# Passes over the edges of a graph network: a fixed instruction order, one-hots for eight chunks at once, lagging additions, more gather buffers

## The chip, the cores and the metric

The kernel runs on one core of one Trainium2 chip, in one launch. The metric is device time in microseconds (us), the median of several runs. A core has five instruction queues, each in order: TensorE (PE, with its weight loads shown as PEld), VectorE (DVE), ScalarE (ACT), GpSimd (POOL) and SyncE (SP). They wait for each other, and for transfers, on semaphores.

## The reference

A graph network on 12,500 nodes with 128 features and 200,000 edges, whose edges come sorted by destination. It has four layers, each followed by a residual and a layer norm. Every layer holds one sum over edges:

```python
num = segment_sum(vals[:, None] * gx[cols], rows)     # layer 0: weighted, by source
agg = segment_sum(feats[src] * norm[:, None], dst)    # layer 1: then a mixture of 64 experts
h   = segment_sum(xs[s], d)                           # layer 2
agg = segment_sum(x[src], dst)                        # layer 3: then two small matrices
```

For every edge a row of 128 (in layer 0, 129) numbers is fetched by the index of one end and added to the row of the other end. The kernel scales the rows of the table, and the sums, by the nodes' own factors outside of these passes; only layer 0 has a weight for each edge. Layer 0's pass also counts the edges that each node receives.

## The kernel before, in words

Nodes lie on partitions, 128 to a node tile, 98 tiles. In its first 2769 us the kernel groups the edges by the node tile of their source, and by that of their destination, and makes *chunks*: 128 edges, one on each partition, whose sums all go to one node tile. There are 1664 chunks in each grouping, so 6656 chunk steps in the four passes. For each chunk it holds the row to gather for every edge (`row`), the edge's place within the node tile (`loc`) and the tile's offset in the table of sums (`off`).

A pass is one call of `edge_sums`. The steps of one chunk, with their lines:

- POOL issues an indirect DMA (L386) that gathers 128 rows from DRAM into the buffer `g`, one of 16 in the pool `gat`. [...]
- In layer 0 alone, ACT multiplies the rows by their weights into `ms` (L390), a ring of `NM` = 8.
- DVE makes a one-hot (L394): a 128x128 matrix that has a 1 where the edge's place is the column, by comparing `iota` with one number for each partition. It has 4 buffers in the pool `hot`.
- PE multiplies the one-hot with the rows (L396), in fp32, which the trace records as two weight loads and two matmuls, into one of 6 PSUM tiles. The product has the sum of each node's edges in the node's own row.
- DVE adds the PSUM tile to the sums `ACC` (L398), at an offset that it has in a register. The offsets are loaded four at a time (L380).

In layer 0 each four chunks are followed by the counting of received edges: DVE makes one-hots `lo` and `hi` for four blocks at once (L402, L405), in tiles of the pool `hot` too, and PE multiplies them (L408) into one PSUM tile that is summed up through the pass.

The program is written chunk by chunk, in the order above. A scheduler sets the order of each engine's instructions. On DVE it puts the one-hot of a chunk some three to four chunks ahead of that chunk's addition, so that in the steady state the queue goes: addition, one-hot of a later chunk, addition, one-hot, and so on. A pool gives its buffers in turn: the gather waits until the matmul (in layer 0, ACT's product) that read its buffer 16 chunks back is done, the one-hot until the matmul four one-hots back is done, and the matmul until the addition that read its PSUM tile six back is done. Before the first chunk of a pass the sums are set to zero (L367, 10.68 us of DVE).

The rest of the kernel (layer norms, the experts between the second and third pass, batch norm) isn't touched by the change.

Of the kernel before, what the change touches and what calls it, by code (L numbers as in the profile page):

```python
# [20 lines left out]
N = 12500                   # nodes; node n lies on partition n % 128 of node tile n // 128  # L21
D = 128
NT = 98                     # node tiles
NP = NT * P
LAST = N - (NT - 1) * P     # nodes in the last tile
E = 200000                  # edges
EC = 1564                   # edges per partition, as loaded
EP = P * EC
NBLK = EP // P              # blocks of 128 edges
NK = 13  # L30
NCH = NK * P                # chunks: a block of edges and a node tile that it reaches
PAD = NP                    # behind every node tile
W0 = D + 2                  # columns of the sums: features, weight sum, edge count
NE = 64                     # experts
# [5 lines left out]
SL = TT * NTT               # rows per expert  # L40
# [3 lines left out]
GM = 7                      # node tiles per group  # L44
# [3 lines left out]
def gnn_kernel(ctx: ExitStack, tc: tile.TileContext, a, out: bass.AP):  # L48
# [6 lines left out]
    # ---- constants  # L55
# [34 lines left out]
    # ---- edges by destination, in chunks: row to gather, place within the node tile  # L90
# [19 lines left out]
    # ---- small helpers on per-node numbers  # L110
# [23 lines left out]
    def bc(v, n):  # L134
        return v[:, :, None].to_broadcast([P, v.shape[1], n])
# [19 lines left out]
    # ---- the edges, grouped by the node tile of their source, and of their destination  # L155
# [4 lines left out]
    def chunks(pool, pps, cum, i, off):  # L160
        """The blocks of edges that each node tile reaches; for each chunk its tile and its block."""
# [46 lines left out]
    def rank_and_store(hi, hv, cum, pack, pos_i, i):  # L208
        """Counting sort by node tile: each edge's place, and its row stored there."""
# [38 lines left out]
    def take_chunks(wk, pps, tl, blk_i, i, row, loc, wgt):  # L248
        """The chunks' edges, one per partition; in a packed row are source, destination, weight."""
        key = i             # grouped by source (0) or by destination (1)  # L250
# [22 lines left out]
    with tc.tile_pool(name="ea", bufs=1) as pa, tc.tile_pool(name="eps", bufs=1, space=PSUM) as pps, \  # L273
# [28 lines left out]
        for i, hi, off in ((0, s_hi, s_off), (1, d_hi, e_off)):  # L302
            hv = pa.tile([P, NT + 2], F32, name=f"hv{i}")
            V.memset(hv, 0.0)
            if i == 1:
                # destinations out of the order of their node tiles
# [13 lines left out]
        # hyperbolic points: table rows are gamma * x_hyp and gamma - 1  # L320
# [26 lines left out]
        # destinations that come grouped by node tile are stored as they are; others are ranked first  # L347
# [11 lines left out]
    # ---- sums over the edges of each node: gather rows, add by a one-hot product  # L359
    def edge_sums(ACC, table, row, loc, off, wgt=None):  # L360
# [3 lines left out]
        with tc.tile_pool(name="gat", bufs=16) as gp, tc.tile_pool(name="hot", bufs=4) as hp, \  # L364
                tc.tile_pool(name="msg", bufs=1) as mp, tc.tile_pool(name="eps", bufs=6, space=PSUM) as ep, \
                tc.tile_pool(name="ops", bufs=1, space=PSUM) as op_:
            V.memset(ACC, 0.0)  # L367
            NM = 8
# [10 lines left out]
            for c0 in range(0, NCH, 4):  # L379
                _, at = nc.values_load_multi_w_load_instructions(  # L380
                    off[0:1, c0:c0 + 4], engines=[mybir.EngineType.DVE], min_val=0, max_val=(NT - 1) * W0,
                    skip_runtime_bounds_check_because="clamped to the last node tile on the chip")
                for i in range(4):
                    c = c0 + i
# [8 lines left out]
                    oh = hp.tile([P, P], F32, name="oh")  # L393
                    V.tensor_scalar(oh, iota, loc[:, c:c + 1], None, op0=OP.is_equal)  # L394
                    ps = ep.tile([P, cols], F32, name="ps")
                    T.matmul(ps, oh, m, start=True, stop=True)  # L396
                    o = ACC[:, ds(at[i], cols)]
                    V.tensor_tensor(o, o, ps, OP.add)  # L398
                if weighted and c0 < EC:
                    # edges that each node receives  # L400
                    lo = hp.tile([P, 4, P], BF16, name="lo")
                    V.tensor_tensor(lo, bc(d_lo[:, c0:c0 + 4], P),  # L402
# [376 lines left out]
```

## Time and profile before

| | |
|---|---|
| median of 3 runs | 14288.24 us (14288.1 to 14297.87) |
| span of the profiled execution, first to last instruction | 14129.2 us |
| median less that span | 159.0 us |
| grouping of the edges, up to the first gather of a pass | 2769 us |
| pass 0 (layer 0, weighted, with the counting) | 2769 to 5215: 2446 us |
| pass 1 (layer 1) | 5385 to 7772: 2387 us |
| experts and batch norm | 7772 to 9086: 1314 us |
| pass 2 (layer 2) | 9086 to 11474: 2388 us |
| pass 3 (layer 3) | 11611 to 13998: 2387 us |
| busy share of the span: PE, PEld, DVE, ACT, POOL | 38%, 27%, 43%, 7%, 62% |
| mean granted TensorE clock | 0.725 |

A line of the groups reads: line of the kernel, engine, operation, output<-inputs, size, count, then busy time in all and the mean of one in ns, then the idle time of the engine just before these instructions, and what ended most of that idle time. "issue" there means that the profile shows nothing that the engine waited for. A line of the timeline reads: start, busy time (both us), engine, line, operation, count, and in brackets the idle time before it with its releaser. Matmuls are pipelined and their ends in the trace are modelled: what tells that a matmul has ended is the instruction that waited for it.

### The profile page before, as it was taken

How to read it: one execution, taken by the hardware profiler on the slowest of the kernel's cores; microseconds unless marked ns; L12 is line 12 of the kernel's file. 1: busy time of each engine (PE TensorE's matmuls, PEld its weight loads, DVE VectorE, ACT ScalarE, POOL GpSimd, SP SyncE). 2: the span in 40 equal slices, each digit the busy share in tenths (PEclk: the TensorE clock that was granted, in tenths of full speed). 3: DMA queues.
4: the chain of work that ended last, by engine and by line, in shares of the span. 5: the costliest groups of instructions: out<-in, count | busy, mean ns of one | idle time of the engine just before them, and what ended most of it. 6: DMA issues, size and time to landing. Idle time of an engine off the chain costs nothing. (4 is left out here: it accounts for less than half of the span.)

```text
span 14129.2 us, 98197 instructions
## 1 busy us (share of the span) xinstructions
PE 5383.5 (38%) x18927; PEld 3844.2 (27%) x18927; DVE 6094.2 (43%) x17635; ACT 1011.7 (7%) x2245; POOL 8749.1 (62%) x8647
## 2 busy tenths in 40 slices
PE   0000000144444433554444385254554425544445
PEld 0000000033333322333333263133333313333334
DVE  9999200144545454333333522533333353333335
ACT  0000000022222220000000121000000000000001
POOL 2888777666666645666666503366666636666663
PEclk9999999999999997555555697555555555555556
DMA  1000000122222211111111143111111111111111
GB/s 48 8 1 1 1 1 1 63 79 46 46 46 46 46 37 50 46 46 46 47 46 45 40 139 89 41 46 46 46 46 46 46 46 46 47 46 47 46 46 47
DMA packets 502257, 619.52 MB, mean 44 GB/s; under 512 B 171448, under 2 KB 379834, under 8 KB 501532
## 3 DMA queue, kind: packets, MB, share of 16 engines
q0 software_dynamic: 277248, 470.82, 13.9%
q1 hardware_dynamic: 164876, 112.21, 2.5%
q10 hardware_dynamic: 59536, 30.17, 0.8%
q14 instruction: 422, 3.46, 0.1%
q8 instruction: 175, 2.87, 0.1%
HBM read 511.43 MB, written 101.18 MB: 43 GB/s over the span
## 5 line engine op out<-in xcount | busy, mean ns | idle before, releaser
L386 POOL DMA_INDIRECT g<-table,e_row x4992 | 4709.0, 943 | 2943.7 <-PE ps L396 1390.8
L396 PE MATMUL ps<-g,oh 128*128 128x128 f32 x9984 | 3471.6, 480 | 4140.4 <-issue 1703.7
L398 DVE TENSOR_TENSOR ACC<-ACC,ps 128x128 f32 (+1 forms) x6656 | 1915.0, 288 | 5966.0 <-PE ps L396 4069.3
L396 PEld LDWEIGHTS ps<-g,oh 128*128 128x128 f32 x9984 | 2402.4, 311 | 5209.6 <-issue 2658.5
L241 POOL DMA_INDIRECT packed<-pack,src_i x1564 | 1991.2, 1273 | 693.0 <-issue 474.1
L386 POOL DMA_INDIRECT g<-table,s_row x1664 | 1637.5, 984 | 796.5 <-issue 524.7
L394 DVE TENSOR_SCALAR oh<-iota,e_loc 128x128 f32<-128x128 f32 x4992 | 1440.9, 297 | 3.9 <-DMA table<-tb 3.1
L396 PE MATMUL ps<-ms,oh 128*128 128x130 f32 x3328 | 995.1, 457 | 664.0 <-issue 366.3
L396 PEld LDWEIGHTS ps<-ms,oh 128*128 128x128 f32 x3328 | 778.0, 321 | 812.6 <-issue 555.3
L260 PE MATMUL tp<-ident,g 128*128 128x128 f32 x65 | 21.7, 442 | 2124.7 <-DVE g L257 2110.1
L390 ACT ACTIVATE ms<-g,s_w 128x129 f32<-128x129 f32 x1664 | 646.7, 401 | 1793.5 <-PE ps L396 824.7
L260 PEld LDWEIGHTS tp<-ident,g 128*128 128x128 f32 x65 | 11.3, 200 | 2135.1 <-DVE g L257 2098.0
L256 DVE COPY g<-gt 128x384 f32<-128x384 f32 x26 | 17.3, 666 | 1250.9 <-DMA gt<-packed,blk_i 1250.7
L654 POOL DMA_INDIRECT yk<-ybuf,come x196 | 188.3, 961 | 593.4 <-DMA ybuf<-ye 533.7
L394 DVE TENSOR_SCALAR oh<-iota,s_loc 128x128 f32<-128x128 f32 x1664 | 435.3, 292 | 0.2
L408 PE MATMUL d_ps<-hi,lo 128*128 128x98 bf16 x1564 | 189.6, 271 | 634.4 <-DVE hi L405 411.6
L408 PEld LDWEIGHTS <-lo 128*128 128x128 bf16 x1564 | 144.1, 124 | 714.5 <-issue 422.0
L233 DVE TENSOR_TENSOR_SCAN inc<-keep,oh 128x1683 f32<-128x1683 bf16 x92 | 336.9, 3662 | 2.5
L598 POOL DMA_INDIRECT buf<-ACC,goi x196 | 197.4, 1007 | 146.7 <-issue 92.5
L238 DVE TENSOR_REDUCE pos<-oh 128x17 f32<-128x1683 f32 x92 | 285.1, 3099 | 2.5
L402 DVE TENSOR_TENSOR lo<-d_lo,iota_b 128x512 bf16<-128x512 bf16 x391 | 267.7, 685 | 0.0
L636 PE MATMUL ph<-bT,w 128*128 128x392 f32 x512 | 215.5, 524 | 71.7 <-DVE bT L630 66.3
(305 smaller groups left out, 3791.3 us busy)
## 6 DMA issues: line engine op xcount, KB each, us to landing
g<-table,e_row POOLq DMA_INDIRECT x4992
g<-table,s_row POOLq DMA_INDIRECT x1664
buf<-zero SPq DMA_DIRECT2D x56, 448.0 KB
xt<-buf ACTq DMA_DIRECT2D x64, 392.0 KB
ybuf<-ye SPq DMA_DIRECT2D x64, 392.0 KB
packed<-pack,src_i POOLq DMA_INDIRECT x1564
w<-in_L_gnn_W SPq DMA_DIRECT2D x128, 128.0 KB
table<-tb SPq DMA_DIRECT2D x28, 448.0 KB
```

Source lines behind the costliest of these rows:

```text
L233: V.tensor_tensor_scan(inc.rearrange("p b k -> p (b k)"), keep.rearrange("p b k -> p (b k)"), oh.rearrange("p b k -> p (b k)"), 0.0, OP.mu ...
L238: V.tensor_reduce(pos, oh.rearrange("p b k -> p k b"), AX.X, OP.add)
L241: st = G.indirect_dma_start(out=rows, out_offset=bass.IndirectOffsetOnAxis(ap=pos_i[:, k:k + 1], axis=0), in_=pack[:, k, :], in_offset=None)
L386: G.indirect_dma_start(out=g, out_offset=None, in_=table[:, :], in_offset=bass.IndirectOffsetOnAxis(ap=row[:, c:c + 1], axis=0))
L390: S.activation(m[:, 0:width], g, AF.Copy, scale=wgt[:, c:c + 1])
L394: V.tensor_scalar(oh, iota, loc[:, c:c + 1], None, op0=OP.is_equal)
L396: T.matmul(ps, oh, m, start=True, stop=True)
L398: V.tensor_tensor(o, o, ps, OP.add)
L402: V.tensor_tensor(lo, bc(d_lo[:, c0:c0 + 4], P), iota_b[:, None, :].to_broadcast([P, 4, P]), OP.is_equal)
L408: T.matmul(d_ps, lo[:, i, :], hi[:, i, :], start=(c0 + i == 0), stop=(c0 + i == EC - 1))
L598: st = G.indirect_dma_start(out=buf[:, :], out_offset=bass.IndirectOffsetOnAxis(ap=goi[:, i, k:k + 1], axis=0), in_=A3[:, t0 + i, 0:D], in ...
L636: T.matmul(ph[:, 0:HALF], w1[:, j * P:(j + 1) * P], bT[:, q * HALF:(q + 1) * HALF], start=True, stop=True)
```

## The change

Only `edge_sums` changes in what it does; elsewhere comments alone go.

- The order of DVE, PE, ACT and POOL inside the pass is the written one (`manual_schedule`), no longer the scheduler's.
- One-hots: one `tensor_tensor` makes those of eight chunks (128 x 8 x 128), from `loc` and `iota`, both spread to that shape, where a `tensor_scalar` made one. The pool `hot` has four tiles of eight. The groups 0 and 1 are made ahead of the first chunk; group g+2 is made at the first chunk of group g.
- An addition stands four chunks behind its matmul in DVE's order (`LAG`). The offsets are still loaded four at a time, before the first addition that needs them.
- The counting's one-hots have a pool of their own (`cnt`, two of each), and the counting of four blocks stands ahead of the four chunks, not behind them.
- 32 gather buffers, not 16; 7 PSUM tiles, not 6; a ring of 12 weighted products, not 8.

The instruction lists of the two kernels show on DVE, per eight chunks: one one-hot instruction; in layer 0 `lo`, `hi`; an offset load and four additions; in layer 0 `lo`, `hi`; an offset load and four additions. POOL's gathers are the same in number and order and differ in what they wait for. PE has the same matmuls, with the counting's ahead of the chunk's own.

```diff
-        with tc.tile_pool(name="gat", bufs=16) as gp, tc.tile_pool(name="hot", bufs=4) as hp, \
-                tc.tile_pool(name="msg", bufs=1) as mp, tc.tile_pool(name="eps", bufs=6, space=PSUM) as ep, \
+        with tc.tile_pool(name="gat", bufs=32) as gp, tc.tile_pool(name="hot", bufs=4) as hp, \
+                tc.tile_pool(name="cnt", bufs=2) as cp, \
+                tc.tile_pool(name="msg", bufs=1) as mp, tc.tile_pool(name="eps", bufs=7, space=PSUM) as ep, \
...
-            NM = 8
+            NM = 12
...
-            for c0 in range(0, NCH, 4):
-                _, at = nc.values_load_multi_w_load_instructions(
-                    off[0:1, c0:c0 + 4], engines=[mybir.EngineType.DVE], min_val=0, max_val=(NT - 1) * W0,
+            def hots(g):
+                t = hp.tile([P, NB, P], F32, name="oh")
+                V.tensor_tensor(t, bc(loc[:, g * NB:(g + 1) * NB], P),
+                                iota[:, None, :].to_broadcast([P, NB, P]), OP.is_equal)
+                return t
+
+            def count(c0):
+                lo = cp.tile([P, 4, P], BF16, name="lo")
+                V.tensor_tensor(lo, bc(d_lo[:, c0:c0 + 4], P),
+                                iota_b[:, None, :].to_broadcast([P, 4, P]), OP.is_equal)
+                hi = cp.tile([P, 4, NT], BF16, name="hi")
+                V.tensor_tensor(hi, bc(d_hi[:, c0:c0 + 4], NT),
+                                iota_b[:, None, 0:NT].to_broadcast([P, 4, NT]), OP.is_equal)
                 for i in range(4):
+                    T.matmul(d_ps, lo[:, i, :], hi[:, i, :], start=(c0 + i == 0), stop=(c0 + i == EC - 1))
+
+            LAG = 4
+            with tc.manual_schedule(engines={mybir.EngineType.DVE, mybir.EngineType.PE,
+                                            mybir.EngineType.Activation, mybir.EngineType.Pool}):
+                made = {g: hots(g) for g in (0, 1)}
+                sums, at = {}, {}
+
+                def add(c):
+                    if c % 4 == 0:
+                        _, at[c // 4] = nc.values_load_multi_w_load_instructions(
+                            off[0:1, c:c + 4], engines=[mybir.EngineType.DVE], min_val=0, max_val=(NT - 1) * W0,
...
+                    o = ACC[:, ds(at[c // 4][c % 4], cols)]
+                    V.tensor_tensor(o, o, sums.pop(c), OP.add)
+
+                for c in range(NCH):
+                    if c % NB == 0 and c // NB + 2 < NG:
+                        made[c // NB + 2] = hots(c // NB + 2)
+                    if weighted and c % 4 == 0 and c < EC:
+                        count(c)
                     g = gp.tile([P, width], F32, name="g")
...
-                    oh = hp.tile([P, P], F32, name="oh")
-                    V.tensor_scalar(oh, iota, loc[:, c:c + 1], None, op0=OP.is_equal)
                     ps = ep.tile([P, cols], F32, name="ps")
-                    T.matmul(ps, oh, m, start=True, stop=True)
-                    o = ACC[:, ds(at[i], cols)]
-                    V.tensor_tensor(o, o, ps, OP.add)
-                if weighted and c0 < EC:
-                    lo = hp.tile([P, 4, P], BF16, name="lo")
...
+                    T.matmul(ps, made[c // NB][:, c % NB, :], m, start=True, stop=True)
+                    sums[c] = ps
+                    if c >= LAG:
+                        add(c - LAG)
+                for c in range(NCH - LAG, NCH):
+                    add(c)
```

More of the change, by code (lines that the diff above doesn't have):

```diff
@@ L357, in gnn_kernel @@
         take_chunks(wk, pps, info[1][3], info[1][4], 1, e_row, e_loc, None)
+    NB = 8
+    NG = NCH // NB
     def edge_sums(ACC, table, row, loc, off, wgt=None):
@@ L378, in edge_sums @@
                 d_ps = op_.tile([P, NT], F32, name="d_ps")
-            for c0 in range(0, NCH, 4):
-                _, at = nc.values_load_multi_w_load_instructions(
-                    off[0:1, c0:c0 + 4], engines=[mybir.EngineType.DVE], min_val=0, max_val=(NT - 1) * W0,
-                    skip_runtime_bounds_check_because="clamped to the last node tile on the chip")
-                for i in range(4):
-                    c = c0 + i
+            def hots(g):
[3 more added lines that the diff above has]
+                return t
@@ new lines, in edge_sums @@
+            LAG = 4
[7 more added lines that the diff above has]
+                            off[0:1, c:c + 4], engines=[mybir.EngineType.DVE], min_val=0, max_val=(NT - 1) * W0,
+                            skip_runtime_bounds_check_because="clamped to the last node tile on the chip")
+                    o = ACC[:, ds(at[c // 4][c % 4], cols)]
[5 more added lines that the diff above has]
+                        count(c)
@@ L392, in edge_sums @@
                         m = g
-                    oh = hp.tile([P, P], F32, name="oh")
-                    V.tensor_scalar(oh, iota, loc[:, c:c + 1], None, op0=OP.is_equal)
                     ps = ep.tile([P, cols], F32, name="ps")
-                    T.matmul(ps, oh, m, start=True, stop=True)
-                    o = ACC[:, ds(at[i], cols)]
-                    V.tensor_tensor(o, o, ps, OP.add)
-                if weighted and c0 < EC:
-                    lo = hp.tile([P, 4, P], BF16, name="lo")
-                    V.tensor_tensor(lo, bc(d_lo[:, c0:c0 + 4], P),
-                                    iota_b[:, None, :].to_broadcast([P, 4, P]), OP.is_equal)
-                    hi = hp.tile([P, 4, NT], BF16, name="hi")
-                    V.tensor_tensor(hi, bc(d_hi[:, c0:c0 + 4], NT),
-                                    iota_b[:, None, 0:NT].to_broadcast([P, 4, NT]), OP.is_equal)
-                    for i in range(4):
-                        T.matmul(d_ps, lo[:, i, :], hi[:, i, :], start=(c0 + i == 0), stop=(c0 + i == EC - 1))
+                    T.matmul(ps, made[c // NB][:, c % NB, :], m, start=True, stop=True)
[4 more added lines that the diff above has]
+                    add(c)
             if weighted:
```

## The prediction, made before the changed kernel ran

> **What bounds the kernel now.** I began with the table of busy time cut into stretches, taken from the first gather to the last addition of each of the four passes over the edges. Its columns are the stretch, its length, busy time (and instructions) of PE, PEld, DVE, ACT and POOL, the granted TensorE clock, the DMA share and GB/s.
>
> ```profile
> 2769.00:5215.00 2446.00, 1147.73 (x4892) 919.00 (x4892) 1201.56 (x4116) 647.97 (x1665) 1637.51 (x1664) 1.00 0.23 56
> 5385.00:7772.00 2387.00, 1146.29 (x3328) 798.45 (x3328) 817.77 (x3324) 0.00 (x0) 1570.04 (x1665) 0.53 0.18 46
> 9086.00:11474.00 2388.00, 1185.91 (x3328) 804.68 (x3328) 808.40 (x3329) 0.00 (x0) 1569.46 (x1664) 0.52 0.18 46
> 11611.00:13998.00 2387.00, 1139.44 (x3328) 799.24 (x3328) 815.97 (x3326) 0.00 (x0) 1569.83 (x1664) 0.51 0.18 46
> ```
>
> The passes are 9608 of the 14129 us of span. No engine fills one: POOL is at 66%, DVE at 34 to 49%. 2387/1664 is 1.43 us a chunk, 2446/1664 is 1.47.
>
> Next the costliest groups, to see who waits:
>
> ```profile
> L386 POOL DMA_INDIRECT g<-table,e_row x4992 | 4709.0, 943 | 2943.7 <-PE ps L396 1390.8
> L396 PE MATMUL ps<-g,oh 128*128 128x128 f32 x9984 | 3471.6, 480 | 4140.4 <-issue 1703.7
> L398 DVE TENSOR_TENSOR ACC<-ACC,ps 128x128 f32 (+1 forms) x6656 | 1915.0, 288 | 5966.0 <-PE ps L396 4069.3
> L386 POOL DMA_INDIRECT g<-table,s_row x1664 | 1637.5, 984 | 796.5 <-issue 524.7
> L402 DVE TENSOR_TENSOR lo<-d_lo,iota_b 128x512 bf16<-128x512 bf16 x391 | 267.7, 685 | 0.0
> ```
>
> The addition waits for the matmul, the gather too (its buffer is free only when the matmul 16 chunks back is done). A gather takes 0.943 us and starts 1.25 us after the last where nothing holds it (9196.83 and 9198.08), so POOL's own pace is 1.25, and 0.18 us a chunk is lost to PE. The timeline of the steady state shows a tempting cause:
>
> ```profile
> 9199.29 0.29 DVE L398 TENSOR_TENSOR ACC<-ACC,ps 128x128 f32 x1 [1.75 <-PE ps L396]
> 9199.49 0.29 DVE L394 TENSOR_SCALAR oh<-iota,e_loc 128x128 f32<-128x128 f32 x1
> ...
> 9199.84 0.80 PE L396 MATMUL ps<-g,oh 128*128 128x128 f32 x2 [1.45 <-issue]
> 9200.73 0.29 DVE L398 TENSOR_TENSOR ACC<-ACC,ps 128x128 f32 x1 [0.94 <-PE ps L396]
> ```
>
> Addition, one-hot, matmul, addition: a loop of 1.44 us, just the pace. But the matmul at 9199.84 is not the one that the addition at 9200.73 takes. How far they stand apart is seen early in the pass, some 16 chunks in:
>
> ```profile
> 9106.50 0.76 PE L396 MATMUL ps<-g,oh 128*128 128x128 f32 x2 [0.44 <-DMA g<-table,e_row]
> ...
> 9107.83 0.76 PE L396 MATMUL ps<-g,oh 128*128 128x128 f32 x2 [0.56 <-DMA g<-table,e_row]
> ...
> 9109.08 0.77 PE L396 MATMUL ps<-g,oh 128*128 128x128 f32 x2 [0.49 <-DMA g<-table,e_row]
> ...
> 9110.23 0.77 PE L396 MATMUL ps<-g,oh 128*128 128x128 f32 x2 [0.39 <-DMA g<-table,e_row]
> ...
> 9112.54 0.29 DVE L398 TENSOR_TENSOR ACC<-ACC,ps 128x128 f32 x1 [5.10 <-issue]
> ...
> 9117.44 0.29 DVE L398 TENSOR_TENSOR ACC<-ACC,ps 128x128 f32 x1 [4.42 <-issue]
> ```
>
> Four matmuls start at the gathers' pace, and their sums come only 4.9 us apart. From there each addition is followed by one one-hot and one matmul start, so four stay begun and unfinished: that is where the four one-hot buffers stop. PE thus has work in hand all the time and still gives one chunk each 1.43 us. Then the end of the last pass:
>
> ```profile
> 13986.90 0.94 POOL L386 DMA_INDIRECT g<-table,e_row  x1 [0.30 <-issue]
> ...
> 13989.22 0.29 DVE L398 TENSOR_TENSOR ACC<-ACC,ps 128x128 f32 x1 [0.28 <-PE ps L396]
> ...
> 13989.62 0.28 DVE L398 TENSOR_TENSOR ACC<-ACC,ps 128x128 f32 x1
> ```
>
> Once the last gather is issued, chunks come 0.40 to 0.75 us apart (19 additions in 10 us, 0.53 on average), with the same one-hot buffers and order. So the order is not what keeps PE at 1.43; what it is the profile doesn't name.
>
> [...] the granted clock here is 1.00 in pass 0 and 0.51 to 0.53 in the others with nearly one pace, so the trace does not settle it. [...] gathers take 984 ns in pass 0, where the two-input count one-hots run, and 943 elsewhere. [...]
>
> **The change part by part.**
> One-hots: 6656 tensor_scalars go, 1440.9 + 435.3 = 1876 us of DVE. 832 tensor_tensors of 1024 elements come[...]. DVE per eight chunks is then 1.22 + 8 x 0.29 + two offset loads of some 0.34 = 4.2 us, in pass 0 with 2 x (0.685 + 0.560) 6.7, against 10 us of gathers. DVE doesn't bound; this saving lies beside PE's time and I cost it at nothing. Were DVE in the loop, it would be worth up to the 0.18 us a chunk, until POOL's 1.25 binds.
> Contention: the new one-hots have two SBUF inputs where the old had one. In pass 0 the count one-hots take 1.245 us per four chunks, 0.311 a gather, and the gather is 41 ns longer: 13%. The new ones are 1.224/8 = 0.153 us a gather, so 20 ns. Bounds: nothing, if POOL waits for PE anyway (0.18 us of slack a chunk covers it), and 6656 x 20 ns = 133 us if not. I take nothing.
> Order and lag: the addition trails by four chunks. It waits for a matmul four back, and behind it on DVE stand only one-hots needed eight or more chunks later. In pass 0 the count one-hots stand behind the addition five chunks back, and PE's count matmuls, now ahead of the chunk's own, wait for them: 1.25 us, covered by four chunks in hand (4 x 0.77 at least). One-hots of two groups now follow the 10.7 us clearing of the sums, so a pass's first matmul may be 2.4 us later; gathers go on meanwhile. Nothing for both; 10 us in all if the cover were gone.
> Buffers: the gather waits for the matmul 32 back, not 16. POOL issues as many gathers in the same order; SP's work is the same. PSUM tiles go from 6 to 7. If PE keeps 1.43, POOL still ends waiting for it, only 32 ahead, and 16 more chunks are left for the quick drain after the last gather: 16 x (1.43 - 0.53) = 14.4 us in each of three passes, 16 x (1.46 - 0.72, its drain's pace) = 12 in pass 0. Sum 55.
> Pass 0: its gathers are 1.461 apart against 1.428. With the counts' one-hots no longer between addition and one-hot, the difference may go in part: 0 to 0.033 x 1664 = 55 us; I take 33, some 60%.
> Sum: -55 - 33 = -88. On the profiled execution's own account, the span goes from 14129 to 14041; 159 us lie around the span, and the median of 14288 goes to 14200.
>
> **The rivals.**
> A, *the loop was the bound* (for it: 1.44 us matches, the addition waits 4069 us for PE; against: four matmuls in hand, and the quick drain with the same loop). Then POOL sets the pace: 1664 x (1.249 + 0.01) + 10 = 2105 in three passes, 1664 x 1.284 + 10 = 2147 in pass 0: -282 x 3 - 299 = -1145, 13,145.
> B, *PE and the gathers share something*, so that a gather and a chunk together cost 1.43 whatever the order (for it: PE at 4.9 us a chunk while POOL runs unheld, 1.43 while both go alike, 0.53 when POOL is done). Then neither buffers nor the longer drain gain, and the gather's 20 ns come on the path in every chunk: +133, 14,421. It decides as soon as lengthened gathers no longer hide in waits for PE; above about 13 ns a gather it outweighs my 88 us.
> C, *DVE's fixed order costs*: each eight chunks a 1.22 us one-hot stands before an addition, and PSUM tiles wait. If a fifth of it showed in every group, 832 x 0.24 = +200, 14,490; seven PSUM tiles with a lag of four speak against it.
> That the order isn't as written can be excluded: the instruction lists show DVE, PE and POOL as described.
>
> **How the numbers follow.** My forecast 0.40, A 0.25, B 0.25, C 0.10. The forecast's own range is 14,130 to 14,270 (drain and pass 0 at both ends). A reaches to 13,090 if pass 0 comes to 1.25 too; B ends at 14,440 with 10 us at the starts. Leaving out the ends of A and most of C, 13,090 to 14,440 holds 8 in 10 or more; both signs are in it. About 0.2% (29 us) is what a measurement can tell. Faster: A, and most of the forecast (0.33), less for what B's price may eat: 0.57. Same: the forecast's upper end and B's lower: 0.13. Slower: the rest of B, C: 0.30.
>
> **What would show it.** Right: gathers in the steady state still 1.43 us apart and waiting for PE, some 32 ahead; the drain after a pass's last gather near 17 us in place of 10; passes near 2373; the addition still waiting for PE. POOL's mean near 963 ns shows the contention, on the path or not. Wrong towards A: gathers 1.25 to 1.28 apart with no wait for PE, passes near 2105. Wrong towards B: passes above 2400, with gathers longer. Towards C: PE waiting for one-hots or PSUM, DVE with little idle time.

## The result, and the profile after

The changed kernel takes 14360.36 us (median of four runs, 14356.54 to 14368.98) where the kernel before takes 14288.17: a ratio of 1.0051, 95% interval [1.0037, 1.0065]. It is slower, by 72 us. The forecast was 14,200, faster; the time lies inside the wide range, on the other side.

The first profile of the kernel before spans 14129 us while its timed runs take 14288. The prediction took the 159 us for time around the span. They are not: the changed kernel's profiled execution spans 14354.7 us and took 14356.5, so 1.8 us lie around a span, and the first profile was simply of a shorter execution than those timed. Below, the changed kernel is therefore set beside a second profile of the kernel before, which spans 14234.7 us (timed on that chip at 14,235).

| us | before, second profile | changed |
|---|---|---|
| first gather of pass 0 | 2777.7 | 2903.1 |
| pass 0 (first gather to last addition) | 2480.2 | 2465.2 |
| pass 1 | 2402.9 | 2410.8 |
| pass 2 | 2403.8 | 2416.3 |
| pass 3 | 2404.8 | 2406.4 |
| the four passes | 9691.7 | 9698.7 |

The passes, which the change rewrote, are the same within 0.1%, and the difference stands ahead of them, in a stage whose code is not touched. The two columns come from different comparisons, though, and passes differ between these by more than 0.1%. Side by side, in one comparison, 72 us were lost; as 125 are lost ahead of the passes, some 50 must have been gained behind that point. The runs with late zeros below find 44 to 46. The costliest groups of the changed kernel:

```profile
L421 POOL DMA_INDIRECT g<-table,e_row x4992 | 4945.8, 991 | 2774.7 <-issue 918.7
L413 DVE TENSOR_TENSOR ACC<-ACC,ps 128x128 f32 (+1 forms) x6656 | 1919.0, 288 | 6435.5 <-PE ps L429 2997.0
L241 POOL DMA_INDIRECT packed<-pack,src_i x1564 | 2104.5, 1346 | 693.6 <-issue 474.7
L421 POOL DMA_INDIRECT g<-table,s_row x1664 | 1710.6, 1028 | 737.4 <-issue 486.9
L386 DVE TENSOR_TENSOR oh<-e_loc,iota 128x1024 f32<-128x1024 f32 x624 | 771.5, 1237 | 3.2 <-DMA table<-tb 3.1
```

The gathers are longer by some 45 ns (943 to 991, 984 to 1028), and still the passes are not. The one-hots take 1237 ns in passes 1 to 3 and 1224 in pass 0. The prediction's 1.224 us for them names no run; an estimate from the first profile of the kernel before gives nearly the same: fp32 instructions of two SBUF inputs take 619 ns at 128x448 (L557) and 1086 at 128x896 (L709), by a straight line 1219 at 128x1024. The line that matters is L241, the scatters that group the edges by source: 1346 ns on average, 1273 in the first profile of before. The table of stretches shows where. Before, second profile:

```profile
1500.00:1740.00 240.00, 0.00 (x0) 0.00 (x0) 0.00 (x0) 0.00 (x0) 182.00 (x191) 1.00 0.02 1
1800.00:2600.00 800.00, 0.00 (x0) 0.00 (x0) 0.00 (x0) 0.00 (x0) 606.67 (x635) 1.00 0.02 1
```

and changed:

```profile
1500.00:1740.00 240.00, 0.00 (x0) 0.00 (x0) 0.00 (x0) 0.00 (x0) 182.05 (x191) 1.00 0.29 99
1800.00:2600.00 800.00, 0.00 (x0) 0.00 (x0) 0.00 (x0) 0.00 (x0) 625.87 (x572) 1.00 0.02 1
```

In the second stretch POOL is alone in both kernels. Before, it does 635 scatters in 800 us, 1.26 us each; after, 572, 1.40 each (957 ns and 1095 ns of busy time, and the same 0.30 between). In the first stretch, up to 1740, both do 191. What the changed kernel has in that stretch, and before has not, is the DMA share of 0.29 at 99 GB/s. The timeline of SP's queue names it, first before, then changed:

```profile
2792.76 71.28 SPq L377 DMA_DIRECT2D buf<-zero  x56
```

```profile
1492.71 68.59 SPq L381 DMA_DIRECT2D buf<-zero  x56
```

These are the zeros of a buffer that a later stage fills, 56 writes of 448 KB. They stand in `edge_sums`, at the start of pass 0. My reading is that in the kernel before their tile lies where an earlier stage's tiles lay, so that its memset waits until that stage is done, and that with the larger pools ahead of it the tile lies in memory that nobody used. The trace has no addresses; two experiments below that change the pools alone bear it out. It does show the times: DVE sets the tile at 1491.8 where it did at 2791.8, and the writes go 1300 us earlier, in the midst of the scatters.

For the passes, the collision foreseen in the prediction is plain in the changed kernel's timeline: a gather that starts while a one-hot runs takes 1.88 us in place of 0.94.

```profile
5547.11 1.22 DVE L386 TENSOR_TENSOR oh<-e_loc,iota 128x1024 f32<-128x1024 f32 x1
5547.27 1.88 POOL L421 DMA_INDIRECT g<-table,e_row  x1 [0.30 <-issue]
...
5549.45 0.94 POOL L421 DMA_INDIRECT g<-table,e_row  x1 [0.30 <-issue]
```

Such gathers (over 1.2 us) are 6.7% of those of passes 1 to 3, with 1.64 us on average; the others keep 0.944. It matters which of the two starts first. A gather that starts 0.1 to 0.8 us into a one-hot ends 0.82 us after the one-hot's end (to 0.01), as here (5549.15 against 5548.33); the 316 gathers that were already running when a one-hot started keep 0.943.

### The profile page after: what moved, and what is told of

Its sections match the earlier page's. It is cut to its first block, busy times and chain, and to the rows that moved or that the text cites. A ratio compares the mean times of both kernels' runs of the same rounds, so it can differ in the third digit from the quotient of the medians.

```text
span 14354.7 us, 91445 instructions
## 1 busy us (share of the span) xinstructions
PE 5101.2 (36%) x18927; PEld 3728.2 (26%) x18927; DVE 5726.5 (40%) x11811; ACT 979.8 (7%) x2245; POOL 9173.3 (64%) x8647
## 5 line engine op out<-in xcount | busy, mean ns | idle before, releaser
L421 POOL DMA_INDIRECT g<-table,e_row x4992 | 4945.8, 991 | 2774.7 <-issue 918.7
L429 PE MATMUL ps<-g,oh 128*128 128x128 f32 x9984 | 3352.5, 469 | 4328.3 <-issue 1844.0
L429 PEld LDWEIGHTS ps<-g,oh 128*128 128x128 f32 x9984 | 2338.9, 304 | 5342.0 <-issue 2836.1
L241 POOL DMA_INDIRECT packed<-pack,src_i x1564 | 2104.5, 1346 | 693.6 <-issue 474.7
L421 POOL DMA_INDIRECT g<-table,s_row x1664 | 1710.6, 1028 | 737.4 <-issue 486.9
L429 PE MATMUL ps<-ms,oh 128*128 128x130 f32 x3328 | 881.6, 432 | 288.9 <-ACT ms L425 130.6
L386 DVE TENSOR_TENSOR oh<-e_loc,iota 128x1024 f32<-128x1024 f32 x624 | 771.5, 1237 | 3.2 <-DMA table<-tb 3.1
L425 ACT ACTIVATE ms<-g,s_w 128x129 f32<-128x129 f32 x1664 | 615.3, 398 | 1843.2 <-remote 904.4
L386 DVE TENSOR_TENSOR oh<-s_loc,iota 128x1024 f32<-128x1024 f32 x208 | 254.4, 1224 | 0.0
L145 ACT ACTIVATE ln_sq<-ln_zc 128x896 f32<-128x896 f32 x56 | 53.2, 950 | 2636.0 <-DVE ln_zc L143 2538.5
```

Of the source, the lines that this page charges most:

```text
L241: st = G.indirect_dma_start(out=rows, out_offset=bass.IndirectOffsetOnAxis(ap=pos_i[:, k:k + 1], axis=0), in_=pack[:, k, :], in_offset=None)
L386: V.tensor_tensor(t, bc(loc[:, g * NB:(g + 1) * NB], P), iota[:, None, :].to_broadcast([P, NB, P]), OP.is_equal)
L421: G.indirect_dma_start(out=g, out_offset=None, in_=table[:, :], in_offset=bass.IndirectOffsetOnAxis(ap=row[:, c:c + 1], axis=0))
L425: S.activation(m[:, 0:width], g, AF.Copy, scale=wgt[:, c:c + 1])
L429: T.matmul(ps, made[c // NB][:, c % NB, :], m, start=True, stop=True)
```

## The experiments

Three questions were put: is it the early zeros that lose the time; do one-hots and buffers do anything in the passes; and what holds a chunk to 1.43 us. Ratios are to the kernel before, run on the same chip in turn.

**The kernel before, again.**

> The kernel before, unchanged, for a second profile. The first one spans 14129 us where the timed runs take 14288. If the difference lies in the grouping of the edges, the first gather of a pass starts near 2903 us here as in the changed kernel, not at 2769, and the passes are 2446 and 2387 again (to 3 us). If it lies in the passes, these are some 40 us longer each. POOL's gathers should take 943 ns in passes 1 to 3.

Measured: 14236.59 us, first gather at 2777.7, passes 2480 and 2403 to 2405, gathers 944 ns. So the stage ahead is as in the first profile, and the passes are some 17 us longer each (35 for pass 0): passes differ that much between executions in different comparisons, the stage ahead by 9 us.

**One-hots with one SBUF input, in the changed kernel.**

```diff
-                V.tensor_tensor(t, bc(loc[:, g * NB:(g + 1) * NB], P),
-                                iota[:, None, :].to_broadcast([P, NB, P]), OP.is_equal)
+                for j in range(NB):
+                    V.tensor_scalar(t[:, j, :], iota, loc[:, g * NB + j:g * NB + j + 1], None, op0=OP.is_equal)
```

> The changed kernel, but each tile of eight one-hots is made by eight tensor_scalar instructions (one SBUF input) where one tensor_tensor (two SBUF inputs) made it. Theory 1, contention: the two-input one-hots lengthen the gathers (991 ns against 943), and this is what the change lost. Then the gathers are at 943 ns again, the passes come to 2387 or less, and the time to 14,200 to 14,290. Theory 2, buffers and lag: more work in flight is what costs. Then the gathers are at 943 but the passes stay near 2410, and the time near 14,360.

Measured: 14351.91, ratio 1.0084 [1.0067, 1.0101]. The gathers are at 946 ns again, the first gather at 2903.1, the passes 9692 in sum, as before's on that chip. Contention is not what the change lost, and theory 2 named the wrong thing too: the passes cost nothing here, and all of the 117 us stand ahead of them (2903.1 against 2777.7).

**16 gather buffers in the changed kernel** (`bufs=16` for `gat`).

> The changed kernel with 16 gather buffers as before. Theory 1, contention: nothing changes, 14,360 within 30, gathers near 990 ns. Theory 2, buffers: the passes come back to 2387 and the time to 14,290. Theory 3, PE's own pace with a drain at the end: 16 fewer chunks are left for the drain, 14,400 to 14,420.

Measured: 14304.04, ratio 1.0051 [1.0034, 1.0068]; first gather 2902.7, passes 2447, 2396, 2398, 2394. The ratio is that of the changed kernel, so this run alone shows no difference between 16 and 32 buffers. Theory 3, by which 16 fewer chunks for the drain would cost 40 to 60 us, is not borne out: 32 buffers are no gain.

**Every second gather left out.**

```diff
+                    if c % 2 == 0:
                         g = gp.tile([P, width], F32, name="g")
```

> The changed kernel with every second gather left out: odd chunks take the rows of the even chunk ahead, so the sums are not the reference's. Everything else is the same. PE's own pace: the passes stay near 2400 us (1.43 a chunk). Shared cost of gather and chunk: by the three rates of the prediction (1.17 us of something per gather, 0.25 per chunk) 0.84 a chunk, passes near 1400. The loop or POOL alone: 0.63 to 0.8 a chunk, passes of 1050 to 1350.

Measured: passes 1 to 3 take 1253 to 1255 us, 0.754 a chunk. Pass 2 in the table of stretches, with 3328 matmul records (1664 chunks) and 832 gathers:

```profile
6976.00:8232.00 1256.00, 856.42 (x3328) 661.33 (x3328) 704.20 (x1875) 0.00 (x0) 881.72 (x832) 0.67 0.17 44
```

PE's own pace of 1.43, the ground of the forecast, falls: PE does two chunks in the time of one. The figure lies in the expectation's last range, the loop or POOL alone (0.63 to 0.8), and under rival B's 0.84. The gathers are 1.47 apart, of which 1.37 are POOL's own (1.06 busy, as 19% of them are lengthened by one-hots, and 0.305 between); it pauses longer before only 9% of them. So POOL all but sets the pace here, and that 1.47 is near 1.43 may be chance.

**Late zeros: the pool of the zeros first.** The changed kernel, with its pools in another order:

```diff
-        with tc.tile_pool(name="gat", bufs=32) as gp, tc.tile_pool(name="hot", bufs=4) as hp, \
-                tc.tile_pool(name="cnt", bufs=2) as cp, \
-                tc.tile_pool(name="msg", bufs=1) as mp, tc.tile_pool(name="eps", bufs=7, space=PSUM) as ep, \
+        with tc.tile_pool(name="msg", bufs=1) as mp, tc.tile_pool(name="gat", bufs=32) as gp, \
+                tc.tile_pool(name="hot", bufs=4) as hp, tc.tile_pool(name="cnt", bufs=2) as cp, \
+                tc.tile_pool(name="eps", bufs=7, space=PSUM) as ep, \
```

> The changed kernel with one thing moved: the pool that holds the weighted products and the zeros stands first among the pools of the pass, so that its memory is again what an earlier stage must free, and the two memsets and the 56 writes of zeros come after the grouping of the edges as they do in the kernel before. Theory 1, the early zeros: the grouping's scatters are at 957 ns again to their end, the first gather of a pass starts near 2780 us and not 2903, and the time falls by some 120 us, to within 0.2% of the kernel before on the same chip. Theory 2, the passes themselves lost the time: nothing changes but the start, and the time stays 0.5% or more above the kernel before.

**The converse: only 32 gather buffers, in the kernel before** (`bufs=32` for `gat`; the zeros move early of themselves).

> The kernel before with 32 gather buffers and nothing else of the change. The larger pool moves the memory of the zeros, and their memsets come early here too. Theory 1, the early zeros: first gather near 2903 us, +110 to +130 us, a ratio of 1.007 to 1.009, with passes as they were (2480, 2403 by three on the second chip; 0 to 10 longer each). Theory 2, early zeros don't matter and the one-hots and the fixed order cost: a ratio of 0.998 to 1.002.

**Late zeros by order.** The changed kernel with its memory as it is, and the memset and writes of zeros put behind the first two groups of one-hots:

```diff
                 made = {g: hots(g) for g in (0, 1)}
+                if weighted:
+                    V.memset(zero, 0.0)
+                    for r in range(0, DUMP // P * D, step):
+                        Y.dma_start(bz[:, r:r + step], zero)
```

> The changed kernel with its own memory, but the zeros are set and written after the one-hots of the first two groups, so after the grouping of the edges; the memset of the weighted products stays early. Theory 1a, the early writes are what slows the scatters: first gather near 2780 us, scatters at 957 ns to their end, a ratio of 0.996 to 0.999 to the kernel before. Theory 1b, the place in memory or the early memset: first gather near 2903 us again and a ratio near 1.005.

Measured, for these three:

| kernel | zeros written from | first gather | passes, sum | ratio |
|---|---|---|---|---|
| late zeros, pool first | 2799 | 2784 | 9655 | 0.9967 [0.9954, 0.9979] |
| before, 32 buffers | 1492 | 2905 | 9736 | 1.0113 [1.0096, 1.0130] |
| late zeros, by order | 2796 | 2780 | 9679 | 0.9970 [0.9959, 0.9982] |

The stretch of scatters from 1800 to 2600 us shows the two speeds again, first in the kernel before with 32 buffers, then with late zeros by order:

```profile
1800.00:2600.00 800.00, 0.00 (x0) 0.00 (x0) 0.00 (x0) 0.00 (x0) 625.88 (x572) 1.00 0.02 1
```

```profile
1800.00:2600.00 800.00, 0.00 (x0) 0.00 (x0) 0.00 (x0) 0.00 (x0) 607.33 (x633) 1.00 0.02 1
```

So theory 1 holds from both sides, and by order alone, with the memory unchanged: early zeros cost some 120 us in these comparisons, and without them the changed kernel is 0.3% faster than the kernel before. Where those 44 to 46 us are gained is not shown, for no profile of the kernel before was taken in these comparisons. The kernel before with 32 buffers lost more than its expectation allowed (1.0113 against 1.007 to 1.009). Part of the rest is seen in its drains, which grow (86 us in sum against 50) while its gathers in passes 1 to 3 stay 1.438 to 1.439 apart: 16 more chunks at the end are added, not saved.

**Late zeros, and 16 buffers; late zeros, and one-hots with one input.**

> The changed kernel with late zeros (its pool first) and with 16 gather buffers. With 16 buffers and early zeros the passes were 62 us shorter in sum than in the changed kernel (9636 against 9699, on different chips); if 32 buffers cost that, this runs 20 to 60 us faster than the kernel with late zeros and 32 buffers (14,197 beside a kernel before of 14,243): a ratio of 0.993 to 0.996. If the buffers don't matter: 0.996 to 0.998.

> The changed kernel with late zeros and with one-hots by eight tensor_scalars. If the longer gathers (986 ns against 946) cost nothing, because POOL waits for PE anyway: within 15 us of the kernel with late zeros, a ratio near 0.997. If they are on the path (rival B), 20 ns x 6656 = 133 us less at most: a ratio of 0.988 to 0.994.

Measured in one comparison: 14185.41, ratio 0.9956 [0.9939, 0.9972], with 16 buffers; 14243.72, 0.9993 [0.9984, 1.0001], with 32 and one-input one-hots; 14210.78 with 32 and the two-input ones (the row above). So here 16 buffers are 25 us better than 32, though the intervals of the two ratios overlap, and the two-input one-hots, whose gathers are longer (991 against 947 ns in passes 1 to 3), are 33 us better than the one-input ones. The row above puts the zeros late by order and these two by the pool; the two ways differ by 0.03% in their ratios. With early zeros the two-input one-hots were better too (1.0051 against 1.0084). The first of these kernels beats both kernels in these comparisons.

**Gathers alone; gathers and matmuls apart.** In passes 1 to 3, first only the gathers; then all of it, but with the matmul on a constant tile (`m = iota`), so that it waits for no gather.

> The changed kernel, but passes 1 to 3 hold the gathers alone: no one-hots, matmuls or additions, so the sums stay zero. If POOL sets the gathers' pace when nothing holds it: 1.249 us each, 2078 us from the first to the last. If the transfers themselves bound it: 1.43 us each, 2375 us.

> The changed kernel, but in passes 1 to 3 the matmul takes a constant tile where it took the gathered rows: gathers run with nobody reading them, and PE waits for none. The sums are not the reference's. If PE and the gathers share something (rival B), both stay slow together: the additions of a pass take near 1664 x 1.2 to 1.43 = 2000 to 2390 us. If only the dependence between them costs, POOL goes at 1.25 to 1.3 us a gather (passes 2080 to 2160 to the last gather) and PE does its 1664 chunks in 750 to 1300 us. If PE has its own pace of 1.43, additions take 2380 and gathers 2080 to 2160.

Measured: gathers alone are 1.383 to 1.386 us apart. The table of stretches for pass 1 shows two paces, 161 in the first 200 us (1.24), then 1465 in 2050 us (1.40):

```profile
5540.00:5740.00 200.00, 0.00 (x0) 0.00 (x0) 0.00 (x0) 0.00 (x0) 151.23 (x161) 0.50 0.18 53
5780.00:7830.00 2050.00, 0.00 (x0) 0.00 (x0) 0.00 (x0) 0.00 (x0) 1603.65 (x1465) 0.50 0.16 47
```

It is the slow scatters' pace, and comes here without any writes of zeros: 188 or 189 gathers after the other engines fell silent, in each of the three passes.

With gathers and matmuls apart, the passes are longer, not shorter: 2962 to 2986 us. Additions and gathers of pass 1 in the timeline:

```profile
7000.45 1.09 POOL L421 DMA_INDIRECT g<-table,e_row  x1 [0.30 <-issue]
7000.86 0.29 DVE L413 TENSOR_TENSOR ACC<-ACC,ps 128x128 f32 x1 [4.62 <-remote]
...
7001.85 0.95 POOL L421 DMA_INDIRECT g<-table,e_row  x1 [0.31 <-issue]
7003.10 1.24 POOL L421 DMA_INDIRECT g<-table,e_row  x1 [0.30 <-issue]
7004.65 1.10 POOL L421 DMA_INDIRECT g<-table,e_row  x1 [0.30 <-issue]
7006.05 0.96 POOL L421 DMA_INDIRECT g<-table,e_row  x1 [0.30 <-issue]
7006.46 0.29 DVE L413 TENSOR_TENSOR ACC<-ACC,ps 128x128 f32 x1 [5.31 <-remote]
```

One chunk is done in the time of four gathers, 5.6 us, with nothing between the two to wait for, and seven matmuls in hand. (It starts faster: 62 to 104 additions in the first 100 us of a pass, then 18 in each 100.) After the last gather the rest takes 0.56 us a chunk (1299 DVE instructions in 650 us, of which eight in nine are additions):

```profile
5600.00:7830.00 2230.00, 316.51 (x796) 199.27 (x796) 171.90 (x449) 0.00 (x0) 1714.93 (x1610) 0.50 0.17 47
7840.00:8490.00 650.00, 525.35 (x2307) 422.85 (x2307) 482.31 (x1299) 0.00 (x0) 0.29 (x1) 0.76 0.01 1
```

So in this run the chunks are held while POOL issues gathers without a pause; whether by the issuing or by the transfers isn't separated. How far this explains the 1.43 of the kernels as they are is not shown. There POOL waits longer than its 0.305 us before only some of the gathers of passes 1 to 3 (38% in the kernel before, 24% in the changed one), about one addition starts in each such wait, and the others start while POOL is at work. And with every second gather left out POOL hardly paused (before 9% of them), and yet two chunks went by in each 1.47 us. An unbroken issue alone is then not enough.

**What is held?** The same without additions, and the same with additions at fixed places:

```diff
-                    o = ACC[:, ds(at[c // 4][c % 4], cols)]
+                    o = ACC[:, ds(at[c // 4][c % 4], cols)] if weighted else ACC[:, (c % 98) * D:(c % 98) * D + cols]
```

> As the kernel with gathers and matmuls apart, and in passes 1 to 3 the additions are left out too, so DVE makes one-hots alone and the sums stay zero. If it is PE that is held while POOL issues without a pause, one-hots (each waits for the matmuls of four groups back) still come about 8 x 5.3 = 42 us apart until the last gather. If it is DVE's additions that are held, PE runs ahead at 0.4 to 0.8 us a chunk, and one-hots come 3 to 6 us apart.

> As the kernel with gathers and matmuls apart, but the additions of passes 1 to 3 go to fixed places, without offsets from registers. The sums are not the reference's. If the offsets in registers are what holds the additions while POOL issues: the 5.3 us a chunk are gone, additions of a pass within 700 to 1300 us. If PE is in a slow state: 5.3 us a chunk again until the last gather, passes near 2960 to the last addition.

Measured: without additions PE does the 1664 chunks of pass 1 in 360 us, 0.22 each, while gathers go on beside it:

```profile
5542.00:5900.00 358.00, 357.07 (x3198) 356.88 (x3196) 252.99 (x211) 0.00 (x0) 302.49 (x182) 1.00 0.13 35
```

With additions at fixed places, 5.6 us a chunk as before (additions at 7002.46, 7008.07, 7013.66). So neither PE's matmuls as such nor the offsets in registers are held; it takes the additions. One-hots still pass between DVE and PE without them, one for eight chunks, 1.79 us apart. Whether the hold lies in the additions themselves or in the exchange of a PSUM tile for each chunk that comes with them isn't separated: both were left out together.

**PE kept busy.** The changed kernel with late zeros, 16 buffers, and one, three or five matmuls of constants behind each chunk's in passes 1 to 3:

```diff
+                    if not weighted:
+                        for _ in range(3):
+                            T.matmul(w_ps, ones_b, wz, start=True, stop=True)
```

> The same with one such matmul behind each chunk's. Slow state by idleness: part of the gain of three, or none if one isn't enough (passes 2100 to 2400). Otherwise 2400 or somewhat more.

> The changed kernel with late zeros and 16 gather buffers, and in passes 1 to 3 three matmuls of constants (bf16, 512 columns, into a PSUM tile of their own that nobody reads) behind each chunk's matmul. If PE falls into a slow state because it stands idle most of the time, work that never waits keeps it out of it: PE no longer holds the gathers, and a pass takes what POOL needs, 1.25 to 1.385 us a gather, 2090 to 2310 us in place of 2400, the whole 13,300 to 13,930. If PE's pace doesn't depend on how busy it is: no change, or longer by the added matmuls (3 x 0.21 to 0.43 us a chunk, passes up to 2700).

Measured: 14154.73 with one, beside a kernel before of 14140; 14223.74 with three, ratio 1.0057 [1.0040, 1.0073], passes of 2419 to 2425. With three, pass 1 reads:

```profile
5369.00:7789.00 2420.00, 1899.26 (x8320) 1086.62 (x8320) 705.51 (x1870) 0.00 (x0) 1662.22 (x1664) 0.84 0.18 46
```

PE is busy for 1899 of 2420 us, its clock 0.84 on average where it was 0.52 in pass 1 of the changed kernel, and the gathers are 1.45 apart. Three added matmuls take 0.81 us at 7006.91 and 1.48 at 7004.26. An idle PE, or its low clock, is not the cause of the pace. What the prediction left unsettled on the clock is settled by timed runs as well: 18 executions of the kernel before in one comparison have a mean granted clock of 0.63 (ten) or 0.725 (eight), and the medians of the two groups agree within 2 us.

> As with three added matmuls, but five behind each chunk's, so that PE has about 1.29 us of work for each chunk at full clock (0.87 with three, 0.21 for each further one), as much as POOL needs for a gather, and hardly ever waits. If chunks are held only when PE has stood idle (clock 0.5): the clock stays near 1.00, the holds are gone, and a pass takes 1664 x 1.30 = 2160 to 2250 us, the whole 13,450 to 13,750. If chunks are held whatever PE does: passes of 2420 us or more, the whole 14,220 or more.

> As the kernel with gathers and matmuls apart, and with three added matmuls behind each chunk's. PE waits for nothing but PSUM tiles here, so it is always busy. If the holds come of an idle PE: 0.9 us a chunk while POOL issues, additions of a pass done in 1450 to 1600 us. If they come of POOL's work alone: 5.3 us a chunk until the last gather again.

Measured: 13148.99 with five, ratio 1.0147 [1.0130, 1.0164], PE busy for 2166 of 2170 us of pass 1 at a granted clock of 1.00 (1.30 a chunk); but the kernel before took 12955.58 beside it, 8 to 9% less than in all the comparisons above. There chunks weren't held: with gathers and matmuls apart the additions came 0.87 us apart while POOL issued. (In passes 1 and 3 that ends after some 925 chunks. My reading is that DVE's queue then has an instruction of the next stage that waits for the last gather, so that this order stops the chunks and no hold does. For 1340 us POOL is alone there, and its gathers keep 1.25 us.) So these two can't tell whether a busy PE lifts the hold where there is one.

**The changed kernel once more.**

> The changed kernel, unchanged, once more. In the last comparison the kernel before took 12,956 us where it had taken 14,140 to 14,290: there the chunks were not held, and POOL set the pace. If chunks are held on this chip (kernel before at 14,140 or more): first gather near 2903 us, passes near 2410, a ratio of 1.004 to 1.007. If they are not held (kernel before near 12,960): passes are POOL's, with gathers of 991 ns and not 943 on their way to the end, near 1664 x 1.297 = 2160 each against some 2085, and with the early zeros a ratio of 1.02 to 1.035.

Measured: no hold here either. The kernel before took 12939.16, the changed one 13382.83: a ratio of 1.0339 [1.0321, 1.0356]. Its groups and passes:

```profile
L421 POOL DMA_INDIRECT g<-table,e_row x4992 | 5202.5, 1042 | 2022.2 <-PE ps L429 893.2
L429 PE MATMUL ps<-g,oh 128*128 128x128 f32 x9984 | 3800.7, 486 | 3393.6 <-DMA g<-table,e_row 2528.3
L241 POOL DMA_INDIRECT packed<-pack,src_i x1564 | 2000.4, 1279 | 693.0 <-issue 473.8
```

```profile
2777.00:4947.00 2170.00, 1427.90 (x4892) 962.54 (x4892) 1123.59 (x2667) 667.78 (x1667) 1649.79 (x1664) 0.51 0.22 51
5117.00:7365.00 2248.00, 1265.59 (x3328) 831.67 (x3328) 700.79 (x1873) 0.00 (x0) 1732.41 (x1665) 0.50 0.19 49
8615.00:10880.00 2265.00, 1272.54 (x3328) 832.65 (x3328) 702.18 (x1875) 0.00 (x0) 1747.71 (x1664) 0.50 0.19 49
11015.00:13253.00 2238.00, 1262.60 (x3328) 830.92 (x3328) 696.60 (x1871) 0.00 (x0) 1722.66 (x1664) 0.50 0.19 49
```

PE now waits for the gathers, the profile's chain puts 39% of the span on transfers, and the pace is POOL's: 1.041 + 0.305 us make the 1.346 between gathers of pass 1. One gather in ten starts just behind a one-hot's start and takes 1.93 us; the others take 0.944. The expectation had counted on 991 ns on average; it is 1042. In the timeline:

```profile
6011.65 1.22 DVE L386 TENSOR_TENSOR oh<-e_loc,iota 128x1024 f32<-128x1024 f32 x1
6011.77 1.92 POOL L421 DMA_INDIRECT g<-table,e_row  x1 [0.30 <-PE ps L429]
```

The kernel before wasn't profiled there, and no run with one-input one-hots was made. An estimate: its gathers at 0.944 + 0.305, in pass 0 at 0.986 + 0.305, and 10 us of drain make 4 x 10 + 1664 x (3 x 1.249 + 1.291) = 8423 us of passes, and with the 4468 that the changed kernel spends outside of them 12,891, to the 12,939 measured 0.4%. By the same sum the changed kernel's 8916 us of passes are 490 longer, as much as the longer gathers of passes 1 to 3 come to (1664 x 0.294, the sum of 0.097, 0.106 and 0.091), and more than the 444 measured. The early zeros cost nothing there: the writes go at 1492.5, and the scatters keep 1.26 us (635 in 800 us, as before), first gather at 2777.7.

The kernel with five added matmuls bears on this. It does more work and was 234 us faster than the changed kernel here, beside kernels before that differ by 16 us. It has the same one-hots, but its gathers take 996 ns on average, not 1042, because they fall otherwise:

```profile
6000.24 0.95 POOL L426 DMA_INDIRECT g<-table,e_row  x1 [0.31 <-issue]
6000.79 1.22 DVE L391 TENSOR_TENSOR oh<-e_loc,iota 128x1024 f32<-128x1024 f32 x1
6001.50 1.33 POOL L426 DMA_INDIRECT g<-table,e_row  x1 [0.30 <-DMA g<-table,e_row]
```

Here the one-hot starts while a gather runs, which keeps its 0.95, and the next gather starts 0.7 us into it and takes 1.33. In the changed kernel 555 of 624 one-hots have a gather that starts within 0.2 us behind them and takes 1.83 on average. In both the lengthened gather ends 0.82 us after the one-hot. So the contention's price depends on where in the one-hot the gather starts. The two kernels differ in buffers, zeros and matmuls too, but 46 ns for each of 4992 gathers is 230 us, nearly all of the difference.

The record gives chip number 10 both for the second profile of the kernel before (14,235) and, 100 minutes later, for the comparison with five matmuls (12,956). If a number is one chip, the hold comes and goes with time and isn't a property of the chip.

## Why the prediction was wrong

*The buffers' step failed twice*, and with it the sum: 88 us less was forecast, 72 more came. "SP's work is the same" is true of its instructions and false of their time. The pools that grew moved a tile of zeros, by the reading above into free memory, and 56 writes left the start of pass 0 for the middle of the scatters. The sum had no term for it: +125 us at the first gather. And the "quick drain" was no gain. It took PE's 1.43 us a chunk as fixed, so that chunks left for the end were cheap. What the runs show is that the gathers of passes 1 to 3 stay as far apart with 32 buffers as with 16 (1.439 in the kernel before, with either), so a longer drain comes on top: -55 was forecast; against 16 buffers the runs show some +25, and drains of 71 us in sum against 50.

*PE's own pace, the ground of the forecast, fell.* Half the gathers gave 0.754 a chunk; without additions PE did 0.22. The reading that led there was right in its first part: the loop was not the bound, four (now seven) matmuls are in hand, and more one-hots ahead bring nothing. It stopped short at PE, because PE was the engine that all waited for. The clue stood in its own lines, under rival B: a chunk in 4.9 us while POOL went unheld, in 0.53 when it was done.

*Rival B had the right kind of mechanism, and the wrong consequence.* Gather and chunk hinder each other: chunks go at 5.6 us beside gathers that nothing stops, and at 0.56 without them. But where they do, the longer gathers cost nothing: with them the kernel was even 33 us better than with the one-input one-hots. I put the contention at 20 ns a gather, in proportion to the one-hots' busy time; it is 48 where chunks are held and some 97 (1.041 against 0.944) where they aren't. There POOL is the bound, so it is on the path in every gather, as B said, and by the estimate above it makes up the 3.4%. Proportion was the wrong form. The profile of the kernel before had the better one, in pass 0: 396 gathers start at least 0.1 us into a count one-hot and end 0.82 us after it on average, and the 977 that meet none keep 0.946.

*Rival A's world exists, in other comparisons*: 12,939 us for the kernel before, with gathers at POOL's pace by the estimate. Neither the order nor the one-hots brought it about in the comparisons at 14,140 to 14,290.

*Right:* DVE has room to spare (busy for 708 of 2412 us in pass 1); one-hots at 1.22 to 1.24 us; no sign of a cost of order and lag, though no run took them alone. Pass 0 was 7 to 33 us under 2480 in the kernels of this order without added matmuls, beside kernels before of 14,235 to 14,290, where I took 33. The drain was 14 to 18 us where I wrote 17, and POOL's mean did show the contention, 991 ns where I wrote 963. But the passes came to 2406 to 2416 and not to 2373. Rival C got no run of its own; passes as long as before's leave no room for its 200 us. With the zeros put back, the changed kernel is 44 to 46 us faster than before, of the 88 forecast; since the drain's 55 did not come, that is nearness by luck and no sign that the sum was half right. The range's lower end has no sum behind it either: with the drain and pass 0 at 55 each it is 14,178 and not 14,130.

*The 159 us "around the span"* were a difference between executions. The forecast's 14,200 rests on the median, so this moved nothing, but such a gap should have been a warning that executions of this kernel differ by more than their spread in one place shows.

Open stays what holds a chunk. Shown are: only in some comparisons; with gathers and matmuls apart, only while POOL issues, and not without the additions; not register offsets; not PE idle or at half clock (0.50 in passes 1 to 3 of the last run, where nothing is held). Open also is why POOL falls from 0.95 to 1.095 us an indirect DMA some 150 to 190 of them after all else is silent (after the early zeros, and in gathers alone), and never in the scatters of the kernel before. It was seen only in comparisons that hold chunks. So that the early zeros cost 125 us is shown; how 70 us of writes slow scatters for 1000 us after them is not.

## What to carry to other kernels

With larger pools alone, the memset and the writes of zeros ran 1300 us earlier here: look at when each memset and each write of the changed program runs, in stages that the diff doesn't touch too, and compare the two profiles stage by stage before explaining a difference by what was rewritten. When an engine has work in hand and still keeps a pace, don't call it the engine's own until its supplier has been halved: one run with every second gather left out would have said more than the profile (0.754 us a chunk where it had been 1.43). Don't call an instruction that lengthens another engine's work free for having cost nothing where that engine waits: gathers of 991 ns against 947 cost nothing where chunks were held, and by the estimate above 3.4% where POOL set the pace. And don't price such a meeting by an average: sort the pairs in the trace by which of the two started first, and by how far in.

## What the runs showed of the hardware

- The kernel before took 12,939 to 12,956 us in two comparisons and 14,140 to 14,290 in the others. For the changed kernel, profiled in both, 783 us of the difference are in the passes, 125 in the early zeros' stage and 63 in the experts' stage between passes 1 and 2. With gathers and matmuls apart, a chunk then took four gathers (5.6 us) while POOL issued without a pause, and 0.56 us after its last gather.
- A gather on POOL that started 0.1 to 0.8 us into a DVE one-hot with two SBUF inputs ended 0.82 us after that instruction (one-hots of 128x1024, 1.22 us, in the changed kernel in both kinds of comparison and with five matmuls; the count's one-hots in the kernel before). One already running when the one-hot started kept its 0.94. With one-hots of one SBUF input the gathers of passes 1 to 3 took 946 and 947 ns in two runs, where they took 991 with those of two.
- Long unbroken runs of indirect DMAs on POOL went from 1.25 to 1.40 us each after 190 to 240 us of silence elsewhere, only in comparisons that hold chunks, and there not in the kernel before's scatters. Where nothing was held, POOL kept 1.25 us through 1340 us alone.
